# A convolution and state-space layer: one step placed a slot later, two blocks written by copies in place of transfers, and a zero state written a slot earlier

## The chip, the cores and the metric

The kernel runs on one core of a Trainium2 chip. The metric is device time in microseconds for one execution of the whole program, lower is better. The core has these engines: TensorE (PE in the profile; PEld is its weight load), VectorE (DVE), ScalarE (ACT), GpSimd (POOL) and SyncE (SP), which here only issues transfers.

## The reference, cut to what matters

The program is four layers on a tensor of 4 images, 128 channels, 64 x 64 points, all in float32: a deformable convolution, the layer of this change, an attention layer with experts, and another one. The second layer computes, for each image (`L` = 4096 points, `C` = 128 channels):

```python
o = einsum('bihw,io->bohw', x, lin1_w) + lin1_b            # 1x1 convolution
o = depthwise 3x3 convolution of o + dw_b
o = silu(o)
s = einsum('bcl,cd->bld', o.reshape(b, c, L), fc_in_w)     # 128 channels -> 32 features
y1 = mamba2(s, weights 0)
y2 = flip(mamba2(flip(s), weights 1))                      # the same, from the end
o = (y1 + y2) @ fc_out_w                                   # then batch norm, 1x1 convolution, sigmoid gate

def mamba2(u):
    z, xBC, dt = split(u @ W_in)
    xs, B, C = split(silu(causal_conv1d(xBC, 4 taps) + conv_b))
    dt = softplus(dt + dt_bias); dA = exp(-dt * exp(A_log))
    for t: h = dA[t] * h + dt[t] * xs[t] * B[t];  y[t] = h . C[t]
    y = (y + D * xs) * silu(z);  y = rms_norm(y) * norm_w;  return y @ W_out
```

The state `h` starts at zero for each image. So the layer is a chain: image, 3x3 convolution, 32 features, and then a scan over the 4096 points from both ends.

## The kernel before, in words

**Tiling.** An image's 4096 points are 32 tiles of 128 points and 8 blocks of 512. A *block* `(n, b)` is what the convolution side works on: 8 rows of image `n`. A *group* `G` is what the scan side works on: four tiles of each direction, `NG` = 8 groups an image, 32 in all. Group `g` of an image reads block `g` for the first direction and block `7 - g` for the other one, so a scan can start only once all blocks of its image are there. The convolution therefore runs 12 blocks ahead (`AHEAD`, L1498).

**The convolution side.** `lines` (L1119) computes the 1x1 convolution of a block's rows (matmul to `pslin`, ACT to `lp`, POOL for the borders). `conv(n, b, k)` (L1141) does tap `k` of the nine: tap 0 is an ACT copy with a scale, the eight others are DVE multiply-adds into a PSUM tile `cop`. `conv_silu` (L1162) is one ACT instruction from `cop` to the SBUF tile `co`, of which there is one buffer (L1172). `features` (L1175) is one matmul of `co` by `fc_in4`, in which the 128 x 32 weight stands four times, so that the result `pss` has the 32 features in each of four bands of partitions. Band `m` is needed `m` points later (the four taps of the causal convolution) in `S4[n % 2]`, the features of one image; two such tiles serve the four images in turn. With `moved` the product goes to `co` by one ACT copy (which writes over the block's input) and from there in four transfers, one a band, on SP's queue (L1188). Without `moved`, a path that only the setup of the layer uses, ACT copies two bands and DVE two, straight from PSUM. For an image's first block POOL first clears three columns at each end of `S4` (L1178).

**The scan side.** `project` and `take` compute the projections of a tile from `S4` (matmuls into `CY`, DVE to the tile `tm`), three groups ahead; `project_c` does so for C (`psc`); `lengths` computes dt in a chain of small ACT, POOL and DVE instructions; `spans` lays out products `ta` on POOL; `masks` and `decay` make of them, by matmuls into `psseg` and `psrow` and by ACT's exponential, the decay matrices `lm` and `Ce`. `state_part`, `update`, `advance`, `weigh`, `within` and `gated` are the scan itself, one tile (one *slot* `j`) at a time: `update` multiplies the state `hst` by `Ce` on PE, `advance` makes the next state on DVE, `weigh` makes `lmc` on DVE, `within` multiplies it on PE, `gated` writes to `Y`. `behind` norms and projects the images that are done, from G = 5 on, in small steps; its transfers to `kept` go on SP's queue too.

**The order.** The main loop (L1539 to L1632) runs over `G` from -3 to 32, and in each group over four slots. All compute engines are wrapped (`InOrder`, L74 to L92), so that each engine runs its instructions in the order of the program text; the profile shows L85 for all of them, and one tells them apart by their tiles. Only SP's transfers are not held by that. So a place in the loop is a place in each engine's queue. What stands where, as far as the change and the prediction touch it:

- slot 0: `conv_silu(last)` on ACT (preceded by the load of the silu table), `conv(now, 0)`, `spans` for direction 0, `silus`, `project_c`, `sums`, `silu_c`, the load of the other table, `decays` (which writes `wd` and `et`)
- slot 1: `masks` and `decay` for direction 0, `spans` for direction 1, and `features(last)`
- slot 2: `masks` and `decay` for direction 1, `turn_b` (the copy to `B`), `state_inputs` (`xw`), `inputs` (`xdt`)
- slot 3: `skips`, `lines(nxt)`, in the last group of an image `project_c` (ahead of time), and `features(last)` where `last` is the first block of image 2 or 3
- every slot: `state_part`, `project`, `update`, `advance`, `weigh`, some taps of `conv(now, k)` (1, 2 and 3; 4 and 5; 6, 7 and 8 over slots 0 to 3), `within`, `take`, `gated`

`last` is block `G + 11` counted over all images, `now` block `G + 12`. So `features` of the first block of image 2 falls in G = 5, that of image 3 in G = 13; their slot is the last one, since image 0's (or 1's) features, in the same tile, are read till then.

In `update`, an image's first slot makes a zero state (four memsets in all, G = 0, 8, 16, 24). Matmul results of the kind `pss`, `psseg`, `psrow`, `psc`, `psb`, `pslin`, `psyt` share one pool of three PSUM buffers (`mm`, L1030).

Of the kernel before, what the change touches and what calls it, by code (L numbers as in the profile page):

```python
# [8 lines left out]
F32 = mybir.dt.float32  # L9
# [8 lines left out]
P = 128  # L18
# [7 lines left out]
G, KP, CG = 8, 9, 16  # L26
# [4 lines left out]
DI = 64  # L31
# [63 lines left out]
class Kernel:  # L95
# [911 lines left out]
    def layer1(self, after):  # L1007
# [7 lines left out]
        nc = plain  # L1015
        NG = 8
        GS = NT // NG
# [3 lines left out]
        with ExitStack() as ctx:  # L1021
# [4 lines left out]
            kp = ctx.enter_context(tc.tile_pool(name="l1k", bufs=2))  # L1026
# [3 lines left out]
            def mm(name):  # L1030
                return pm.tile([P, 512], F32, name=name, tag="mm")
# [61 lines left out]
            nc = InOrder(tc)  # L1093
# [68 lines left out]
            def conv_silu(n, b):  # L1162
                src = cos[n, b]
                own = space(n, b)
                if len(src.shape) == 2:
                    src = src.rearrange("p (r c) -> p r c", c=HW)
                if own:
                    cos[n, b] = own[1]
                elif (n, b) == (0, 5):
                    cos[n, b] = gp.tile([P, 512], F32, name="Ce").rearrange("p (r c) -> p r c", c=HW)  # L1170
                else:
                    cos[n, b] = gp.tile([P, 8, HW], F32, name="co", bufs=1)  # L1172
                nc.scalar.activation(cos[n, b], src, AF.Silu, bias=self.col("dw_b"))

            def features(n, b, moved=True):  # L1175

                s = S4[n % 2]
                if b == 0:  # L1178
                    nc.gpsimd.memset(s[:, 0:3], 0.0)
                    nc.gpsimd.memset(s[:, L:L + 3], 0.0)  # L1180
                ps = mm("pss")
                nc.tensor.matmul(ps, fc_in4, cos[n, b].rearrange("p r c -> p (r c)"), start=True, stop=True)
                if moved:
                    nc.scalar.copy(cos[n, b].rearrange("p r c -> p (r c)"), ps)
                for m in range(4):
                    ms = slice(32 * m, 32 * m + 32)
                    if moved:
                        plain.sync.dma_start(s[ms, b * 512 + m:b * 512 + m + 512],  # L1188
                                             cos[n, b][ms].rearrange("p r c -> p (r c)"))
                    elif m < 2:  # L1190
                        nc.scalar.copy(s[ms, b * 512 + m:b * 512 + m + 512], ps[ms, :])
                    else:
                        nc.vector.tensor_copy(s[ms, b * 512 + m:b * 512 + m + 512], ps[ms, :])
# [43 lines left out]
            def sooner(g):  # L1237


                return g % NG == NG - 1 or g - 2 + AHEAD + 1 >= NB * NG  # L1240

            def silus(g):
                q = groups[g]
                tmf = q.tm.rearrange("p j e -> p (j e)")
                nc.scalar.activation(tmf, tmf, AF.Silu)
# [131 lines left out]
            def block(c, dr, j):  # L1377
                return c[64 * dr:64 * dr + 64, j * P:(j + 1) * P]
# [7 lines left out]
            state, weighted, outs = {}, {}, {}  # L1386

            def weigh(g, j):
                q = groups[g]
                lm = kp.tile([P, 2, P], F32, name="lmc")  # L1390
                nc.vector.tensor_tensor(lm, q.lm[:, :, j, :], CY[j % 2][:, :, 0:P], ALU.mult)
                weighted[g, j] = lm
# [8 lines left out]
            def update(g, j):  # L1401

                q = groups[g]
                if g % NG == 0 and j == 0:
                    state[0] = kp.tile([P, DI], F32, name="hst", bufs=3)
                    nc.vector.memset(state[0], 0.0)
                for dr in range(2):
                    nc.tensor.matmul(CY[j % 2][:, dr, 128:192], block(q.Ce, dr, j), state[0][64 * dr:64 * dr + 64, :],
                                     start=True, stop=False, skip_group_check=True)
# [129 lines left out]
            for G in range(NG + 1 - AHEAD, N + 1):  # L1539
                here = 0 <= G < N  # L1540
                soon = 0 <= G + 1 < N
                later = 0 <= G + 2 < N
                first = 0 <= G + 3 < N
                now = divmod(G + AHEAD, NG) if G + AHEAD < N else None
                nxt = divmod(G + AHEAD + 1, NG) if G + AHEAD + 1 < N else None
                last = divmod(G + AHEAD - 1, NG) if 0 <= G + AHEAD - 1 < N else None

                if later:
                    dts = lengths(G + 2)

                for j in range(GS):
                    if (G, j) in starts:
                        backs.append(behind(*starts[G, j]))
                    if last is not None and j == 0:
                        conv_silu(*last)
                    if now is not None and j == 0:
                        conv(*now, 0)
                    if soon and j == 0:
                        spans(G + 1, 0)
                        silus(G + 1)  # L1560
                    between, behind_it = (((1,), ()), ((2,), (3,)), ((4, 5), ()), ((6,), (7, 8)))[
                        j] if now is not None else ((), ())
                    if here:
                        if j == 0 and G == 0:
                            pairs(0, 0)
                        state_part(G, j)
                    if first:
                        project(G + 3, j)
                    if here:
                        update(G, j)  # L1570
                    if soon and j == 0:
                        if not sooner(G + 1):
                            project_c(G + 1)
                        sums(G + 1)
                        silu_c(G + 1)
                    if j == 0 and (later or soon or here):
                        nc.scalar.preload_act_table_set("natural_log_exp_and_others")
                    if soon and j == 0:
                        decays(G + 1)
                    if later and j == 0:  # L1580
                        next(dts)
                    if here:
                        advance(G, j)
                        weigh(G, j)
                    if later and j:
                        next(dts)
                    if soon and j == 1:
                        masks(G + 1, 0)
                        decay(G + 1, 0)
                        spans(G + 1, 1)  # L1590
                        q = groups[G + 1]
                        nc.gpsimd.tensor_tensor(q.wd, q.wd, q.dt, ALU.mult)
                    if soon and j == 2:
                        masks(G + 1, 1)
                        decay(G + 1, 1)
                        turn_b(G + 1)
                        state_inputs(G + 1)
                    if soon and j == 3:
                        skips(G + 1)
                    if nxt is not None and j == 3:  # L1600
                        lines(*nxt)
                    if later and j == 3 and sooner(G + 2):
                        project_c(G + 2)
                    if last is not None and j == (3 if last[0] > 1 and last[1] == 0 else 1):
                        features(*last)
                    for b in list(backs):
                        if next(b, b) is b:
                            backs.remove(b)
                    for k in between:
                        conv(*now, k)  # L1610
                    if here:
                        within(G, j)
                        if j + 1 < GS:
                            pairs(G, j + 1)
                        elif soon:
                            pairs(G + 1, 0)

                    if first:
                        take(G + 3, j)
                    if here:  # L1620
                        gated(G, j)
                    if soon and j == 2:
                        inputs(G + 1)
                    for k in behind_it:
                        conv(*now, k)
                    for b in list(backs):
                        if next(b, b) is b:
                            backs.remove(b)
            while backs:
                backs = [b for b in backs if next(b, b) is not b]  # L1630
            nc = plain
# [1340 lines left out]
```

## Time and profile before

| | |
|---|---|
| median of 3 runs | 4801.95 us (4800.6 to 4808.87) |
| the profiled execution | 4802.76 us |
| its span | 4800.9 us |
| mean granted TensorE clock | 0.97 |
| the second layer's main loop in the trace | about 890 to 1500 us of the span |
| PE busy in 900 to 1500 us | 565.7 of 600 us |
| DVE, ACT, POOL busy there | 367.3, 395.3, 425.4 us |
| table loads on ACT in 890 to 1500 us | 66, of 1.283 us each |

The span is the time from the first to the last instruction of the profiled execution; the execution's own time is 1.86 us longer. The third and fourth layers take the time from about 1500 us to the end, and nothing in them depends on the order within the second one. In the trace each instruction has a start, a duration and, in brackets, the idle time of its engine ahead of it with what ended this idle time. `CY<-hst,Ce` is `update`'s matmul, `CY<-xdt,lmc` that of `within`, `cop<-lp,cols,cop` a tap of the convolution, `co<-cop,cols` `conv_silu`, `co<-pss` the copy in `features`, `S<-co` its transfers and `S<-pss` the copies that write a block directly.

The starts of `silus` (ACT, `tm<-tm` with 1536 elements) mark off the groups. Measured from one to the next, a group takes:

| G | us |
|---|---|
| 0 to 4 | 17.87, 17.87, 17.79, 18.09, 17.87 |
| 5, 6 | 22.12, 20.92 |
| 7 to 12 | 16.81, 19.83, 16.82, 19.72, 16.76, 19.82 |
| 13, 14 | 22.14, 21.28 |
| 15 to 20 | 16.82, 22.52, 16.81, 19.72, 15.88, 17.80 |

(A group's row is the time from the `silus` in its slot 0 to those in the next group's slot 0: the row of 5 goes from 1005.48 to 1027.60 us.)

### The profile page before, as it was taken

Reading aid. Unit: us, or ns where it says so; the run is one execution under the profiler, and the core shown is the slowest. Engines: PE = TensorE matmul, PEld = TensorE weight load, DVE = VectorE, ACT = ScalarE, POOL = GpSimd, SP = SyncE. Lnnn points to the kernel's source line nnn. Section 1 sums busy time; section 2 is a strip of 40 time slices with the busy share of each in tenths; the row PEclk is TensorE's granted clock in tenths of the full one; section 3 lists DMA queues with packets and bytes.
Section 4 is the critical chain, followed back from the end, with each engine's and each line's share of the span. In section 5 each row is a group of like instructions: output and inputs, shape, how many; then the busy total and the mean of one; then the engine's idle time right before and its main releaser. Section 6 shows DMA issues by size and latency. Waiting matters only on the chain. (4 is left out here: it accounts for less than half of the span.)

```text
span 4800.9 us, 67063 instructions
## 1 busy us (share of the span) xinstructions
PE 4424.1 (92%) x23064; PEld 2411.2 (50%) x23064; DVE 3391.4 (71%) x6475; ACT 3618.5 (75%) x5498; POOL 3117.7 (65%) x3443
## 2 busy tenths in 40 slices
PE   6889987899997899997989999999999999999798
PEld 4778775566774344443434444444444444444344
DVE  5999996666645888855866666766676666665675
ACT  4456553566666777775758999999999999999575
POOL 0234443367783455544887878887888788877488
PEclk9999999999998999998999999999999999999899
DMA  6666773101002000000000000000000000000000
GB/s 213 186 184 188 194 193 82 26 22 30 28 17 90 23 1 1 0 1 1 36 36 1 1 1 1 1 1 1 1 1 1 1 1 1 1 1 1 10 29 34
DMA packets 71704, 196.33 MB, mean 41 GB/s; under 512 B 13940, under 2 KB 17204, under 8 KB 69684
## 3 DMA queue, kind: packets, MB, share of 16 engines
q1 hardware_dynamic: 65924, 175.96, 12.8%
q0 software_dynamic: 2240, 12.85, 1.0%
q8 instruction: 187, 3.06, 0.3%
q10 hardware_dynamic: 3184, 3.08, 0.2%
q14 instruction: 169, 1.38, 0.1%
HBM read 133.23 MB, written 50.74 MB: 38 GB/s over the span
## 5 line engine op out<-in xcount | busy, mean ns | idle before, releaser
L85 POOL TENSOR_TENSOR r<-r 128x512 f32<-128x512 f32 (+1 forms) x1088 | 1348.7, 1241 | 332.4 <-DVE r L85 271.8
L85 DVE TENSOR_TENSOR r<-r,num 128x1024 f32<-128x1024 f32 (+1 forms) x1088 | 975.4, 928 | 599.6 <-PE num L85 495.2
L85 PE MATMUL D<-F,G 32*128 32x512 f32 (+3 forms) x4608 | 1139.2, 573 | 2.1 <-DVE den L85 0.9
L85 PE MATMUL num<-F,G 32*128 32x512 f32 (+3 forms) x4608 | 1057.2, 590 | 6.8 <-DVE r L85 3.9
L85 ACT ACTIVATE r<-r 128x2048 f32<-128x2048 f32 (+4 forms) x610 | 1018.5, 1679 | 51.3 <-POOL r L85 4.7
L85 ACT ACTIVATE r<-D 128x1536 f32<-128x1536 f32 (+1 forms) x544 | 763.6, 1404 | 49.8 <-PE D L85 29.6
L85 PEld LDWEIGHTS D<-F,G 32*128 32x128 f32 x4608 | 484.2, 184 | 373.6 <-issue 235.1
L85 PE MATMUL acc<-r,v 128*128 128x512 f32 (+3 forms) x1152 | 598.1, 606 | 0.7 <-ACT r L85 0.7
L85 POOL TENSOR_TENSOR x<-x 128x512 f32<-128x512 f32 (+2 forms) x320 | 405.4, 1267 | 148.4 <-DVE m L85 66.5
L85 PEld LDWEIGHTS num<-F,G 32*128 32x128 f32 x4608 | 383.3, 183 | 223.4 <-issue 110.7
L85 PE MATMUL pff<-hid,w_ffn_w2T 128*128 128x512 f32 x1024 | 468.6, 600 | 0.0
L85 PE MATMUL pex<-w_expert_w,vT 128*128 128x512 f32 x1024 | 461.4, 598 | 1.6 <-DVE x L85 1.4
L85 POOL TENSOR_TENSOR piece<-v,wt 128x512 f32<-128x512 f32 x160 | 167.6, 1065 | 376.2 <-DVE cum L85 90.0
L85 PEld LDWEIGHTS acc<-r,v 128*128 128x128 f32 x1152 | 174.1, 188 | 382.7 <-issue 180.4
L85 PE MATMUL acc<-ident,pr 128*128 128x128 f32 x2560 | 319.1, 282 | 45.2 <-DVE pr L85 45.2
L85 ACT ACTIVATE x<-pex,gate 128x128 f32<-128x128 f32 x896 | 257.5, 368 | 102.2 <-PE pex L85 76.9
L85 PEld LDWEIGHTS acc<-ident,pr 128*128 128x128 f32 x2560 | 296.0, 146 | 59.9 <-DVE pr L85 58.6
L85 ACT ACTIVATE hid<-phh,cols 128x512 f32<-128x512 f32 x416 | 253.1, 689 | 67.7 <-PE phh L85 67.7
L85 PEld LDWEIGHTS pex<-w_expert_w,vT 128*128 128x128 f32 x1024 | 190.6, 192 | 216.5 <-issue 160.6
L85 PEld LDWEIGHTS pff<-hid,w_ffn_w2T 128*128 128x128 f32 x1024 | 185.0, 191 | 200.9 <-issue 200.9
L85 DVE TENSOR_TENSOR pr<-v,near_w 128x2560 f32<-128x2560 f32 x96 | 270.2, 2815 | 6.2 <-PE acc L85 5.4
L85 DVE SCALAR_TENSOR_TENSOR cop<-lp,cols,cop 128x512 f32<-128x512 f32 x192 | 143.4, 747 | 35.5 <-ACT cop L85 33.4
(502 smaller groups left out, 7656.6 us busy)
## 6 DMA issues: line engine op xcount, KB each, us to landing
v<-tab SPq DMA_DIRECT2D x320, 256.0 KB
oms<-omw SPq DMA_DIRECT2D x32, 432.0 KB
omr<-oms SPq DMA_DIRECT2D x32, 432.0 KB
X<-in_x_dram SPq DMA_DIRECT2D x8, 1024.0 KB
tab<-vb SPq DMA_DIRECT2D x64, 128.0 KB
o<-o SPq DMA_DIRECT2D x32, 256.0 KB
oin<-o SPq DMA_DIRECT2D x32, 256.0 KB
kept<-X SPq DMA_DIRECT2D x4, 2048.0 KB
```

Source lines behind the costliest of these rows:

```text
L85: self.last = op(*args, **kwargs)
```

## The change

- The zero state of an image is made in the last slot of the group before it, after `weigh`, and no longer at the head of `update`.
- `features` of a block stands in slot 2 instead of slot 1.
- `features` of the first blocks of images 2 and 3 stays in slot 3, but writes its result by two ACT copies and two DVE copies of 32 x 512 instead of one ACT copy and four transfers.

```diff
             def update(g, j):
 
                 q = groups[g]
-                if g % NG == 0 and j == 0:
-                    state[0] = kp.tile([P, DI], F32, name="hst", bufs=3)
-                    nc.vector.memset(state[0], 0.0)
                 for dr in range(2):
...
                     if here:
                         advance(G, j)
                         weigh(G, j)
+                    if soon and j == GS - 1 and (G + 1) % NG == 0:
+                        state[0] = kp.tile([P, DI], F32, name="hst", bufs=3)
+                        nc.vector.memset(state[0], 0.0)
                     if later and j:
                         next(dts)
...
-                    if last is not None and j == (3 if last[0] > 1 and last[1] == 0 else 1):
-                        features(*last)
+                    if last is not None:
+                        late = last[0] > 1 and last[1] == 0
+                        if j == (3 if late else 2):
+                            features(*last, not late)
```

## The prediction

> **What bounds the kernel now.** The page's first part says who is busy, its slices when; the change lies in slices 8 to 13 (890 to 1500 us).
>
> ```profile
> span 4800.9 us, 67063 instructions
> PE 4424.1 (92%) x23064; PEld 2411.2 (50%) x23064; DVE 3391.4 (71%) x6475; ACT 3618.5 (75%) x5498; POOL 3117.7 (65%) x3443
> ```
>
> PE is the bound by share, but an average over four layers says nothing of this one. The chain of waits goes back only through the last stretch (PE 5% of the span), so it does not reach the second layer. I therefore took the windows view (PE 91.5 to 98.4 of each 100 us from 900 to 1500, 34.3 us idle in all), then the waits of 890 to 1500, for what could be won:
>
> ```profile
> ACT L85 <- DMA S<-co: 10.2, 2, 5.1
> ...
> PE psseg L85 <- issue: 9.4, 2, 4.7
> ...
> PE pss L85 <- ACT et L85: 5.4, 6, 1.0
> ...
> PE psseg L85 <- POOL ta L85: 3.8, 10, 0.8
> ...
> PE CY L85 <- DVE hst L85: 1.9, 2, 0.9
> ```
>
> Columns: us in total, times, longest. Lines one and two are one event, twice: the "late" blocks (2,0) and (3,0). ACT waits 5.1 us for the four transfers out of `co` and, behind it, PE 4.7 us for `silu_c`. Line three is `features`' product in slot 1, six times behind `et`; line five the zero state. Everything else of PE's idle the change does not name. What counts is therefore the time from one group's `silus` to the next's: 17.8 to 18.1 in G=0 to 4, 16.8 (odd G) and 19.8 (even G) in most of 7 to 19, 22.1 and 20.9 in 5 and 6, 22.1 and 21.3 in 13 and 14.
>
> **Part 1: the zero state, one slot sooner.** Four memsets of 112 ns stand ahead of slot 0's `update`; in G=8 and 16 PE waited 0.95 for them (1063.79, 1216.98), in G=0 and 24 not. Moved ahead of the previous slot's taps, the wait goes: **-1.9**. The memset takes 0.11 there, and DVE waits for PE anyway. After G=16's wait the clock fell:
>
> ```profile
> 1028.00:1034.00 6.00, 4.20 (x7) 2.06 (x8) 2.37 (x7) 5.29 (x11) 2.48 (x5) 0.50 0.00 0
> 1215.00:1219.00 4.00, 3.05 (x34) 2.45 (x33) 2.87 (x9) 3.53 (x5) 3.55 (x15) 1.00 0.00 0
> 1219.00:1226.00 7.00, 7.00 (x31) 5.65 (x32) 2.48 (x7) 4.37 (x10) 3.28 (x6) 0.51 0.00 0
> ```
>
> The column after the five engines is the granted clock: 0.51 after 0.95 us of idle, and G=16 lasts 22.52, 2.7 above its neighbours. G=8, with the same wait, kept its clock. I take half of the 2.7, since new waits elsewhere may cause such a stretch as well: **-1.3** (0 to -2.7). The Trainium skill, page "TensorE: Matmul & The Clock Gate", section "HAM oscillation — how this bites in real kernels", lets the clock fall after idle gaps above about 3.4 us: it agrees with the 0.50 behind the 4.7 us gap and not with the 0.51 here. By it this term would be 0, and the sum 1.3 higher.
>
> **Part 2: `features` from slot 1 to slot 2, 22 blocks.** One product (0.96 until the next on PE), one ACT copy (0.57) and four SP transfers move; their count stays.
> - PE, G=0 to 4: the 0.98 behind `et` goes, but group 5, which has nothing in slot 1, shows what is late next: two waits of 0.51 for POOL's `ta`. From the table load ahead of `conv_silu` to slot 2's `within` it takes 10.81 (1002.77 to 1013.58), with the product's 0.96 11.77, against 11.58 in G=3 (966.81 to 978.39). 5 x 0.2: **+1.0** (-1 to +2).
> - The transfers start after slot 2's B copy, some 4.8 us later (978.93 + 0.59 + 0.57 against 975.32). Four issues take 2.4 and the last lands about 1.6 after its end (1023.30, ACT goes on at 1024.90): 4.0 from the copy, 5.3 where one issue is long (1.2 to 2.1 in place of 0.6, in 15 of 22). The next `conv_silu` writes the same `co`. Startup first: in G=-1 the B copy ends at 910.02, so the transfers land about 914.6, the load of G=0 stood at 913.28: +1.3; G=-2 by the same sum about +0.7: **+2** (0 to 4). `project` of group 8 in G=5 reads block (1,7) at 1001.0 and may wait: **+0.7** (0 to 2).
> - The table load ahead of `conv_silu`. Here two kinds of group differ in the trace of before:
>
> ```profile
> 984.90 1.28 ACT L85 ACT_TABLE_LOAD   x1 [1.49 <-issue]
> 986.20 0.69 ACT L85 ACTIVATE co<-cop,cols 128x512 f32<-128x512 f32 x1
> ```
> ```profile
> 1081.66 1.28 ACT L85 ACT_TABLE_LOAD   x1
> 1083.76 0.69 ACT L85 ACTIVATE co<-cop,cols 128x512 f32<-128x512 f32 x1 [0.82 <-DVE cop L85]
> ```
>
> In the first (G=4) the load itself waits for DVE's last tap (`cop`, until 984.83) and the silu follows 1.30 later; in the second (G=9) the load runs under the taps and only the silu waits. In the changed program, as built, the wait for the last tap stands on the load also in G=7, 9, ... 19, seven groups more. There `conv_silu` comes 1.30 later (1083.76 to 1085.06). Behind it on ACT stand `conv`'s copy, `silus` and `silu_c`, behind those `wd`, then POOL's `ta` (3 us), `psseg` of slot 2 and all that PE has after it: 1092.33 to about 1093.1 to 1093.7 for `psseg`, and PE, which had 0.1 us idle in this stretch, can't make it up. 7 x 1.3 = **+9.1** (0 if the wait is met in time, 9.8 at 1.4 each). The Trainium skill, page "ScalarE: Activation LUTs", section "What ACT_TABLE_LOAD costs", speaks harder against the change: about 2.66 us for every switch, a drain of 1.38 included. The trace has 1.30 from load to silu. By the page this term would be 18.6 and the sum 9.5 higher.
> - In the even group after it the load waits for the transfers: copy ends about 1096.2, landed 1100.2, and 1101.5 to 1102 with a long issue. The load must end by 1101.65 to cost nothing, so it is 1.3 late where an issue is long. Six such groups, say half with about 1.0: **+3** (0 to 8).
>
> **Part 3: the late blocks by copies.** Eight transfers go; per block come two ACT copies (setup's row: 2.35 for four) and two DVE copies (2.86 for four) in place of one ACT copy.
>
> ```profile
> 875.26 2.35 ACT L85 COPY S<-pss 32x512 f32<-32x512 f32 x4 [0.17 <-PE pss L85]
> 876.46 2.86 DVE L85 COPY S<-pss 32x512 f32<-32x512 f32 x4 [5.47 <-ACT S L85]
> ```
>
> Setup does the same, and there DVE's copies waited for ACT's (5.47); the built program has that wait in the late blocks too, and both wait for POOL's memset of S. So, in G=5: memset until 1020.89, ACT copies until 1022.07, DVE copies until 1023.5. Behind DVE's copies are queued tap 6 (0.70), `take`, `u`, `y` and the last two taps (1019.60 to 1021.88 now, 2.28): last tap 1026.5, `conv_silu` 1026.5 against
>
> ```profile
> 1019.21 0.59 ACT L85 COPY co<-pss 128x512 f32<-128x512 f32 x1 [0.81 <-PE pss L85]
> 1024.90 1.28 ACT L85 ACT_TABLE_LOAD   x1 [5.10 <-DMA S<-co]
> 1026.19 0.69 ACT L85 ACTIVATE co<-cop,cols 128x512 f32<-128x512 f32 x1
> ```
>
> The table load is hidden now, but what is late next is DVE: the wait moves from the transfers to the taps. PE's idle moves as well: `lmc` at about 1027.0 instead of 1022.4 holds `within`, PE has 4 us of idle there, and `psseg` follows `silu_c` at about 1030 as before (1029.74). POOL's `Y` and `ta` wait for the later `y` and end near 1029: just covered. 2 x 0.3 = **+0.6** (-2 to +3; -7 to -13 in a rival).
>
> **Sum**: -1.9 - 1.3 + 1.0 + 2 + 0.7 + 9.1 + 3 + 0.6 = **+13.2**. The profiled execution took 4802.76 (span 4800.9, 1.86 around it), so 4816.0; the median of the three runs is 0.81 below it: **4815**. By the bounds the case spans 4805 to 4828.
>
> **Rivals.**
> - *The late stalls really go* (the other side: faster). Place: slot 3 of G=5 and 13. If ACT's and DVE's copies don't wait for the memset, or run beside each other, the last tap ends about 1.4 to 2.8 sooner; once PE's idle is short enough to keep the clock, the half-speed stretch 1028 to 1034.7 (2.5 us) goes too: 3.9 to 6.6 each; the groups 5+6 and 13+14 last 43.0 and 43.4 against 36.6 for a usual pair, so 6.4 and 6.8 are the ceiling. With the seven loads hidden as well, -10.5 + 1.0 + 2 + 0.7 - 4.6 = -11.4: **4790**. It decides once the last tap ends before about 1025. For: the transfer wait is the largest stall of the stretch. Against: setup's 5.47.
> - *Both the stalls go and the loads are exposed*: 13.2 - 0.6 - 10.5 = +2.1: **4804**, no change.
> - *The loads stay hidden and the late blocks gain nothing* (DVE's last tap is earlier, since the product leaves slot 1): -1.9 - 2.7 + 1.0 + 2 + 0.7 + 0.6, about 0: **4802**.
>
> **How the numbers follow.** This kernel's measurement can tell about 0.2%, 9.6 us. Forecast 0.5; stalls go 0.17; both 0.13; neither 0.2. The first splits about 0.46 slower by over 9.6 and 0.04 within; the second 0.14 faster and 0.03 within; the rest is within, but for 0.05 that slips to each side. Range 4790 to 4826: it takes in all cases but the ends of the first two; the likeliest case alone is 4805 to 4828.
>
> **What would show it.** Right: in odd groups from G=7 the load's row names DVE's tap and `conv_silu` starts 1.3 after it; as `silus` then come later, it is G=8, 10, 12 and 18 that last about 21.1, not 19.8; no `ACT <- DMA S<-co` of 5 us, but DVE `S<-pss` behind ACT `S` and PE waiting 4 us for `lmc` in G=5 and 13; no PE wait for `hst`; `pss` in slot 2. Wrong: those at 19.8; groups 5 and 13 at 18 to 19 with the clock at 1.0 (first rival); new half-clock stretches of 6 to 7 us, 2.5 each, which I count only against the one at G=16.

## The result, and the profile after

The changed kernel takes 4821.1 us (median of 8 runs, 4816.65 to 4821.87) against 4802.23 us for the kernel before (8 runs beside them): a ratio of 1.0035, 95% interval 1.0027 to 1.0044, so 13 to 21 us slower. The forecast was 4815, within 4790 to 4826.

First the page of the changed kernel, then its waits from 890 to 1500 us (us in all, times, longest), to be read against those of before.

```profile
span 4819.8 us, 67046 instructions
PE 4440.1 (92%) x23064; PEld 2426.2 (50%) x23064; DVE 3396.1 (70%) x6479; ACT 3620.4 (75%) x5500; POOL 3119.1 (65%) x3443
```
```profile
ACT L85 <- DVE cop L85: 25.4, 12, 2.2
...
PE psseg L85 <- POOL ta L85: 15.5, 32, 1.0
...
DVE S L85 <- ACT S L85: 10.7, 2, 5.3
...
ACT L85 <- DMA S<-co: 7.4, 8, 2.2
...
PE CY L85 <- DVE lmc L85: 5.9, 3, 2.9
...
ACT S L85 <- POOL S L85: 5.0, 2, 2.5
```

Before, the same view had these two lines for ACT's table load, beside that of the transfers:

```profile
ACT L85 <- issue: 7.3, 5, 1.5
...
ACT L85 <- DVE cop L85: 3.0, 1, 3.0
```

The shares say nothing: PE has 16 us more of busy time for the same number of instructions. The waits say nearly all. The first line of after was one wait of 3.0 us and is now twelve of 25.4 us: ACT's table load behind DVE's last tap. Five of the twelve (10.3 us) are the loads of G=1 to 5, which waited for this tap before, too, as the five of 7.3 us that the view puts down to "issue". Seven (15.1 us) are new: G=7, 9, 11, 13, 15, 17 and 19. The second was 10 waits of 3.8 us: PE behind POOL's `ta`, which comes later because `silus` does. The other four are the late blocks and the transfers: two waits of 5.1 us for transfers have become two of DVE (5.3), two of ACT (2.5) and two long ones of PE for `lmc` (2.9 and 2.4). `PE <- DVE hst` and `PE pss <- ACT et` are gone.

From one `silus` to the next, in us, by group:

| G | before | after |
|---|---|---|
| -1 | 16.36 | 19.08 |
| 0 to 4 | 17.87, 17.86, 17.79, 18.10, 17.87 | 18.00, 18.00, 17.93, 18.23, 18.01 |
| 5, 6 | 22.12, 20.93 | 22.54, 22.35 |
| 7, 9, 11, 15, 17 | 16.81, 16.82, 16.76, 16.82, 16.82 | 16.69, 16.68, 16.91, 16.68, 16.69 |
| 8, 10, 12, 18 | 19.83, 19.72, 19.82, 19.71 | 21.10, 20.98, 21.10, 21.00 |
| 13, 14 | 22.14, 21.28 | 22.55, 21.73 |
| 16, 19, 24 | 22.52, 15.88, 18.98 | 21.09, 17.60, 17.77 |
| 29 | 16.14 | 16.58 |
| -1 to 29, sum | 560.0 | 570.3 |

The groups that are not listed differ by at most 0.06. The mean granted clock of the whole span is lower as well (0.966 against 0.970), but that is not what makes 8, 10, 12 and 18 longer: no half-clock stretch lies in them in either profile.

One row is the heart of it. ACT at the head of G=9 in the changed kernel, and DVE beside it:

```profile
1094.13 1.28 ACT L85 ACT_TABLE_LOAD   x1 [2.15 <-DVE cop L85]
1095.42 0.69 ACT L85 ACTIVATE co<-cop,cols 128x512 f32<-128x512 f32 x1
```
```profile
1092.52 1.54 DVE L85 SCALAR_TENSOR_TENSOR cop<-lp,cols,cop 128x512 f32<-128x512 f32 x2
```

ACT now idles for 2.15 us and only then loads the table. Before, the load ran in that time and the idle was 0.82. The last two taps end at 1094.06, the silu starts 1.36 later; before it followed the last tap (1083.72) at 1083.76.

The 18.9 us between the two profiled executions are not all of this layer. At the end of its setup (before's 868.3 us, ahead of everything the change touches) the changed kernel was already 5.1 late, at the layer's end (1499.7) 19.4, at the end of all 18.9. So the layer accounts for 14.4 in this pair of executions; the 5.1 is taken up below.

### The profile page after: what moved, and what is told of

It reads as the page before. It is cut to its first block, busy times and chain, and to the rows that moved or that the text cites. A ratio compares the mean times of both kernels' runs of the same rounds, so it can differ in the third digit from the quotient of the medians.

```text
span 4819.8 us, 67046 instructions
## 1 busy us (share of the span) xinstructions
PE 4440.1 (92%) x23064; PEld 2426.2 (50%) x23064; DVE 3396.1 (70%) x6479; ACT 3620.4 (75%) x5500; POOL 3119.1 (65%) x3443
## 5 line engine op out<-in xcount | busy, mean ns | idle before, releaser
L85 ACT ACT_TABLE_LOAD x112 | 143.7, 1283 | 34.3 <-DVE cop L85 25.4
```

The source lines that it names most:

```text
L85: self.last = op(*args, **kwargs)
```

## The experiments

The ratios are against the kernel before, run beside each; its median was 4802.5 in the first set of four and 4806.5 in the second, so the ratios and the groups in the traces are compared, not the medians across sets. The first set is e_slot, e_after_pre, e_mem and e_late. The expectations of the second set were written against about 4802 and are to be read some 4 us higher.

**e_slot: the shift alone.**

```diff
-                    if last is not None and j == (3 if last[0] > 1 and last[1] == 0 else 1):
-                        features(*last)
+                    if last is not None:
+                        late = last[0] > 1 and last[1] == 0
+                        if j == (3 if late else 2):
+                            features(*last)
```

> The shift of features to slot 2 alone (late blocks by transfers in slot 3, zero state as before). My theory, that the shift puts the wait for the last tap on the table load of G=7, 9, ... 19: about 1.3 us longer in each of G=6, 8, 10, 12, 16 and 18, 1.7 in 19, 2.7 at the start (G=-1), 0.7 in G=0 to 4 together, so the loop about 13 us longer and the whole about 4815 to 4823. Rival, that the later transfers are the cost: the same time, but the rows of the table loads name the DMA and not DVE's tap.

Measured: 4818.4 us, ratio 1.0038 (1.0024 to 1.0051). The groups 8, 10, 12 and 18 last 21.09, 21.00, 21.10, 21.00 as in the full change, G=-1 19.09. G=6 and 19 (21.37 and 16.02, 0.4 and 0.1 above before) do not show the 1.3 and 1.7 expected: the 1.7 of the full change was a half-clock stretch (1299.2 to 1302.6) and is 0.2 in its second execution. Two groups without a new wait, G=0 (19.57) and G=22 (19.01), hold half-clock stretches of this execution. Its waits from 890 to 1500 us:

```profile
ACT L85 <- DVE cop L85: 25.3, 12, 2.1
ACT L85 <- DMA S<-co: 19.0, 10, 5.1
```

So the whole loss is the shift's, and the same twelve waits for the tap come with it. The second line is the rival's: ten waits of transfers, of which two are the late blocks' 5.1 us and were there before. Which of the two costs the time, this run does not tell; e_after_pre does.

**e_after_pre: the changed kernel with the table loaded by an instruction of its own.**

```diff
                     if last is not None and j == 0:
+                        nc.scalar.preload_act_table(AF.Silu)
                         conv_silu(*last)
```

> The changed kernel with an explicit load of the silu table at the head of slot 0, so that the load itself waits for nothing and only conv_silu waits for tap and transfers. My theory: the 1.28 us come back in the seven groups, and about 1 us in each of G=0 to 4 and at the start, where the load waited before the change as well: 4804 to 4809. Rival, that the later transfers hold conv_silu: 4818 to 4821, since they land no sooner.

Measured: 4798.5 us, ratio 0.9990 (0.9981 to 0.9999), the loss gone and 4 us beyond, better than the theory's 4804 to 4809. The transfers are where they were (in G=9 the first one is issued 9.8 us after `silus` in both kernels), the load is not. ACT at the head of G=9:

```profile
1080.33 1.28 ACT L85 ACT_TABLE_LOAD   x1
1082.48 0.69 ACT L85 ACTIVATE co<-cop,cols 128x512 f32<-128x512 f32 x1 [0.86 <-issue]
```

Load at once, 0.86 of idle behind it: the row of before again. G=8, 10, 12 and 18 are at 19.81, 19.71, 19.83 and 19.72, each 1.27 to 1.29 below the changed kernel and within 0.02 of before. G=0 to 4, where the load waited before the change too, fall from 18.0 to 16.7. The theory is shown: the price of the shift is the load that it puts behind the tap. The rival is out as the main cause; the transfers' part is what is left: G=-1 stays at 17.03, 0.67 above before.

**e_mem: the zero state alone.** The edit is the first two hunks of the change.

> The zero state a slot sooner alone. My theory: the waits of 0.95 us in G=8 and 16 go, and with them the half-clock stretches in G=16 (2.7 us) and G=24 (1.2 us), so 4797 to 4799. Rival, that half-clock stretches only move to another place: 4800 to 4802, with as much time at half clock as before.

Measured: 4803.4 us, ratio 1.0002 (0.9993 to 1.0011): no change. PE's wait for `hst` is gone and G=8 lasts 19.83 as before. Where about half of it went is seen on PE some 7 us later (two shorter waits, 0.08 and 0.12, stand ahead of this one), in e_mem and then in before:

```profile
1071.12 1.12 PE L85 MATMUL pss<-co,w_fc_in 128*128 128x512 f32 x2 [0.36 <-ACT yT L85]
```
```profile
1070.24 1.12 PE L85 MATMUL pss<-co,w_fc_in 128*128 128x512 f32 x2
```

PE reaches this point early and waits for ACT: in both profiles the product starts 4.90 us after `silus`. `silus`, and with them the group, are set by taps, `conv_silu` and the load on DVE and ACT, and not by PE in slot 0. The half-clock stretches in G=16 and G=24 did not appear in e_mem, but the half-clock time of this layer is as long as before: 61 us from 870 to 1530 us in both profiles, the stretches at its end being longer instead. That is the rival's outcome. That the edit moved them is not shown: e_late, below, lacks the two stretches as well and keeps the old place of the zero state.

**e_late: the late blocks by copies alone.** As in the change, with `features` in slot 1 otherwise.

> The late blocks by copies alone, in slot 3. My theory, that DVE's copies stand ahead of the taps and take the place of the wait for the transfers: G=5 and G=13 within 0.5 us of before, the whole 4801 to 4804. Rival, that the two stalls of 4.7 us go: 6 us less each, 4790.

Measured: 4800.7 us, ratio 0.9997 (0.9988 to 1.0006): no change, and the rival's 4790 is out; G=5 and 13 at 22.55 and 22.54 (before 22.12 and 22.14), G=6 and 14 at 20.75 and 21.04 (20.93 and 21.28). ACT, DVE and PE around the late block in G=5:

```profile
1021.62 1.17 ACT L85 COPY S<-pss 32x512 f32<-32x512 f32 x2 [2.48 <-POOL S L85]
1022.80 1.28 ACT L85 ACT_TABLE_LOAD   x1
1027.40 0.69 ACT L85 ACTIVATE co<-cop,cols 128x512 f32<-128x512 f32 x1 [3.31 <-DVE cop L85]
```
```profile
1022.87 1.40 DVE L85 COPY S<-pss 32x512 f32<-32x512 f32 x2 [5.32 <-ACT S L85]
1024.30 0.76 DVE L85 SCALAR_TENSOR_TENSOR cop<-lp,cols,cop 128x512 f32<-128x512 f32 x1
...
1025.83 1.54 DVE L85 SCALAR_TENSOR_TENSOR cop<-lp,cols,cop 128x512 f32<-128x512 f32 x2
```
```profile
1024.42 1.05 PE L85 MATMUL psyt<-ident,ys 128*128 128x128 f32 x4 [1.44 <-DVE S L85]
1027.93 1.12 PE L85 MATMUL CY<-xdt,lmc 128*128 128x64 f32 x4 [2.46 <-DVE lmc L85]
```

Read as a chain: memset, ACT's copies, DVE's copies, tap 6, the last two taps, silu. The load is hidden and of no use. This kernel keeps the old place of the zero state, and PE still waits 0.95 us for it in G=16 (1218.06), but the stretch from 1219 to 1226 us is at full clock, the column after the five engines:

```profile
1219.00:1226.00 7.00, 6.93 (x53) 5.11 (x49) 3.07 (x8) 6.63 (x13) 5.96 (x10) 1.00 0.00 0
```

So the 0.51 there, in the profile of before, does not follow from this wait alone. e_slot, e_late_set, e_before_pre and e_best keep the wait, too (0.95 in G=16 in each), and none of them has this stretch.

**e_late_set: the same with POOL's memset in slot 2.**

```diff
+                    if last is not None and j == 2 and last[0] > 1 and last[1] == 0:
+                        clear(last[0])
```

`clear` makes the two memsets, which `features` no longer does for these blocks.

> The late blocks by copies alone, with POOL's memset of the edge columns a slot earlier (slot 2), so that ACT's copies wait for the product only. Theory, that the queue of copies, then taps, sets conv_silu: ACT's and DVE's copies and the last tap come about 1.8 us sooner, G=5 and 13 from 22.55 to about 20.8, and less half clock after it: 4796 to 4799. Rival, that PE or POOL hold these groups anyway: within 0.5 us of 22.55, 4800 to 4803.

Measured: 4802.9 us, ratio 0.9995 (0.9986 to 1.0004), inconclusive on the whole, but G=5 and 13 last 20.88 and 20.88, 1.67 less than in e_late, as the chain says. ACT's copies now wait for the product alone, 0.81 us where they waited 2.48 for the memset:

```profile
1023.35 1.16 ACT L85 COPY S<-pss 32x512 f32<-32x512 f32 x2 [0.81 <-PE pss L85]
```

In its profile, half-clock stretches in G=2 (19.37), 4 (19.44), 20 (18.45) and 28 (18.98) took this back; nothing of the edit lies in these groups.

**e_before_pre: the kernel before with the explicit load.** The edit is that of e_after_pre.

> The kernel before (features in slot 1, late blocks by transfers) with an explicit load of the silu table at the head of slot 0. Theory, that a load behind the last tap costs 1.1 to 1.3 us a group: G=0 to 4 go from 17.87 to about 16.75, the odd groups, where the load was hidden already, stay; the start gains about 1: 4795 to 4797. Rival, that the 4 us which the changed kernel with this load gained over the kernel before came from slot 2 and the copies: 4801 to 4803.

Measured: 4798.8 us, ratio 0.9984 (0.9975 to 0.9993). G=0 to 4 are at 16.59, 16.59, 16.51, 16.81 and 16.58, 1.27 to 1.29 below before, more than I expected; G=5 and 13 gain 1.27 to 1.29 as well, since the load no longer waits for the transfers. With slot 2 (e_after_pre) G=0 to 4 take 0.13 to 0.15 more than here. So the gain needs neither slot 2 nor the copies, and the rival is out. It also closes the argument on the change itself: with the load ahead of the wait in both kernels, the changed one (0.9990) is 0.0006 above this one, within their intervals; without it, it is 0.0035 above.

**e_best: explicit load, slot 1, and the late blocks by four ACT copies, none on DVE.**

```diff
-                    elif m < 2:
+                    elif n > 1 or m < 2:
                         nc.scalar.copy(s[ms, b * 512 + m:b * 512 + m + 512], ps[ms, :])
```

with the load of e_before_pre, the copies of e_late and the memset of e_late_set.

> The kernel before with the explicit table load, and the late blocks by four ACT copies and none on DVE, the memset in slot 2. Theory: no copy stands ahead of the taps any more, conv_silu of G=6 and 14 follows the copies and the load some 3.5 to 4 us sooner than with transfers, PE's idle falls below 2.5 us and the clock stays: groups 5+6 and 13+14 last 37 to 38 in place of 43; with the loads of G=0 to 4 hidden 4783 to 4788. Rival, that ACT becomes the bound there (four copies, 2.35 us, and the load): 4793 to 4797.

Measured: 4792.3 us, ratio 0.9974 (0.9964 to 0.9984), the fastest. ACT at the late block of G=5, and the clock behind it:

```profile
1013.33 2.34 ACT L85 COPY S<-pss 32x512 f32<-32x512 f32 x4 [0.81 <-PE pss L85]
1015.69 1.28 ACT L85 ACT_TABLE_LOAD   x1
1016.98 0.69 ACT L85 ACTIVATE co<-cop,cols 128x512 f32<-128x512 f32 x1
```
```profile
1021.00:1028.00 7.00, 6.47 (x23) 3.71 (x21) 1.15 (x5) 4.38 (x12) 2.56 (x5) 0.51 0.07 18
```

The theory's 4783 to 4788 is 0.9960 to 0.9971 of 4802, the rival's 4793 to 4797 is 0.9981 to 0.9990; the result lies between them, and both have a part. `conv_silu` follows the end of `pss` on PE by 3.7 us (copies and load, so ACT is what is late there, as the rival says) and no tap stands in its way: G=5 and 13 last 18.80 each, 3.3 below before, and 5+6 and 13+14 40.8 and 39.1 against 43.0 and 43.4. The clock did not stay, though (0.51), so the 37 to 38 expected was missed.

**e_after_again: the changed kernel once more.**

> The changed kernel once more. If the 4.9 us by which the first layer was later in its profile, ahead of anything the change touches, belong to the program, they are there again; if they are the scatter of one execution, the first layer ends within 2 us of before and the median is about 4816.

Measured: 4821.5 us, ratio 1.0031 (1.0020 to 1.0043). At 868.3 us it was 0.9 behind before, not 5.1; the groups 8, 10, 12 and 18 were 21.11, 21.02, 21.13, 21.01, the loop from G=-1 to 29 took 570.4, and the end was 17.9 behind. The early offset is the scatter of one execution. The median of 4821.5 is no higher than the 4816 expected in that case, since the kernel before was 4 us slower in this set, too: the ratio 1.0031 is 15 us, and 4816 would have been 14. The layer itself was 15.6 longer in this execution.

## Why the prediction was right, step by step

- **The table load, +9.1: right, in mechanism and size.** 1.27 to 1.28 in G=8, 10, 12 and 18, 1.42 in G=6, 0.45 in G=14 (why less there stays open: G=6 holds as long a half-clock stretch, 10.2 us), and in G=16 the same 1.27 (21.09 against the 19.82 that it lasts in e_mem): about 8.3, and 9.3 by the same groups in e_after_again. The sign and most of the size of the result came from reading which instruction bears a wait, in the rows of G=4 and G=9 of before. The Trainium skill, page "ScalarE: Activation LUTs", section "What ACT_TABLE_LOAD costs", gives 1.283 us for the load, which every row here shows, and 2.66 with a drain; no drain is seen: 1.29 from the load's start to the silu's, and 1.27 to 1.29 won back by hiding it.
- **The start, +2: right in kind, too small.** G=-1 took 2.7 more, where I had 1.3: the load that closes it (G=0's) waits 2.20 us for the transfers. Ahead of it the two executions of the changed kernel lost 0.2 and 2.5 more, where I had 0.7. Each had 6.8 us of half clock there and before had none, but e_late and e_late_set had as much and lost nothing, so what made the 2.5 stays open.
- **G=0 to 4, +1.0: measured 0.7**, 0.13 to 0.14 each.
- **The long DMA issues, +3, and `project` in G=5, +0.7: wrong, nothing.** Four issues took 2.4 us in every group of after: the issues of 1.2 to 2.1 us that I carried over from slot 1 did not come along to slot 2. The loads of the even groups from 8 to 18 wait at most 0.6 us for transfers, and `conv_silu` starts on time.
- **The late blocks, +0.6: right.** 0.4 in G=5 and in G=13. The chain was as worked out: the last tap ends 5.7 after the memset in e_late, I had 5.6. e_late_set and e_best show that it is the cause: take 1.7 from its head and the groups lose 1.7; take DVE's copies out of it as well and they lose 3.7 in all (e_best has the explicit load, too, but in these groups the load stands right behind ACT's copies in all three kernels).
- **The zero state, -1.9: wrong, 0.** That PE's wait of 0.95 us in G=8 and 16 goes was true of the wait and not of the time. PE was ahead of the chain that sets these groups; e_mem shows where it waits instead.
- **The clock, -1.3: its cause was wrong.** Two stretches were missing in G=16 and 24 (-2.7 and -1.2), but before's profile is the only one of the ten that has them, and five of the others keep the wait. It was the scatter of one execution.
- **What no term held:** the time behind G=29. The layer's end took 3.9 us more than before in after, and 2.8 in e_after_again, with more time at half clock there than before. That this follows from the change is not shown: the end took 1.1 us more in e_late and 5.5 more in e_mem, too. The loop took 10.3 us more; with the 0.2 ahead of it and this last, unforeseen part the layer comes to 14.4.
- **The sum: in part luck.** The load, the start, G=0 to 4 and the late blocks came to 12.7 together, and 12.7 was forecast. The other four terms were to add 0.5 (3 + 0.7 - 1.9 - 1.3) and were wrong one by one. In their place stand differences in half-clock stretches, none of them shown to follow from the change: 3.9 less in G=16 and 24, 1.7 more in G=19, 0.4 more in G=29 and the 3.9 more at the end. With small differences in other groups (-0.5) that makes 14.4. The bounds of the range, too, come out a little wider from the terms as they stand: 4803 to 4829, not 4805 to 4828.

Of the rivals, the late stalls that "really go" were ruled out by e_late, with or without exposed loads; the loads that stay hidden were ruled out by e_slot.

## What to carry to other kernels

A wait belongs to the instruction that bears it: where a table load is put in ahead of an activation, a move of unrelated work can shift the activation's wait onto the load, and 1.28 us a group come into the open. An explicit load, ahead of the instruction that waits, costs one line and here was worth more than all the moves. And a wait of an engine is worth its time only if that engine ends the group: measure the group from one fixed instruction to the next, and ask what is late next before counting a wait as a gain.

## What the runs showed of the hardware

The granted clock also fell where the idle time of PE was short. In e_best it is 0.51 from 1021 to 1028 us, and the only idle time of PE over 0.3 us that the trace shows in the 15 us ahead is 1.44 us (until 1020.57, for `silu_c`). The wait of 0.95 us in G=16 was followed by half clock in before (0.51 from 1219 to 1226 us), and not in e_slot, e_late, e_late_set, e_before_pre and e_best, which have it, too. The Trainium skill, page "TensorE: Matmul & The Clock Gate", section "HAM oscillation — how this bites in real kernels", names gaps above about 3.4 us: these runs show half clock behind shorter ones, so the single gap does not tell it. What does, stays open.

The length of a transfer's issue goes with its place. In the profiles of the six kernels that have `features` in slot 1, 14 to 18 of the 88 to 96 issues of these transfers on SP took over 1 us (up to 2.1, the others mostly about 0.6); in the four profiles with it in slot 2, none or one, for the same transfers some 4 to 5 us later in the group. What makes them long in slot 1 was not tried.
